# One of v's last two projection products moved by half a key block at the end of each image's fourth head

## The chip, the cores and the metric

The kernel runs on 1 core of one Trainium2 chip. The metric is device time in microseconds (us): the median over runs of the whole program on that core. Before the change it is 3168.52 us (3 runs, 3167.76 to 3169.66).

## The reference, cut to what matters

The input x has 16 images of 512 channels and 32x32 positions (n = 1024), all in float32. Each image goes through group normalisation, a 1x1 convolution to q, k and v, attention with 4 heads of 128 channels over the 1024 positions, a 1x1 convolution of the result, and the residual sum.

```python
xn = ((xg - mu) * rsqrt(var + EPS)).reshape(b, c, h, w) * gamma + beta
q, k, v = split(einsum('oc,bchw->bohw', qkv_w, xn) + qkv_b, 3, axis=1)
q, k, v = to_heads(q), to_heads(k), to_heads(v)        # b, 4 heads, 1024, 128
attn = softmax(einsum('bhnd,bhmd->bhnm', q, k) * dh ** -0.5, axis=-1)
out = einsum('bhnm,bhmd->bhnd', attn, v).transpose(0, 1, 3, 2).reshape(b, c, h, w)
return x + einsum('oc,bchw->bohw', proj_w, out) + proj_b
```

## The kernel before, in words

**The main loop.** `fast_path` (L187) walks over 16 images x 4 heads x 8 key blocks of 128 keys, 512 steps in all (L1245). A step has two halves of 512 queries. In each half TensorE gets the scores of this step (`scores`, L862, written `s<-qk,qk` in the profile), then the weighted sum of the step before (`weighted_sum`, L935, `po<-p,v`), then some projection products taken from a list. ScalarE turns the scores into exponentials (L868, tile `p`), and VectorE adds those up over the key blocks (L881, tile `tot`). The denominators of a head come from `tot` (L890 to L904) in the second step of the next head (the call is at L1257).

**The projections in between.** The projections that feed other heads and the next image are spread over the halves. A projection (q and k for a pair of heads, v, or the output) is a two-level Strassen product (`two_levels`, L539). The outer level gives four groups, `OUTER = ((1, 5), (2, 6), (7, 4), (3,))` (L183), so that groups 0 to 2 do two outer products side by side and group 3 does one. Inside each group stand the seven inner products of `strassen` (L488), in the order 1, 2, 6, 5, 7, 4, 3 (L184). In group 3 an inner product is one 128x256 product, which the trace shows as two matmuls of 256 columns; a score or a weighted sum of a half shows as two matmuls of 512.

**The PSUM tiles of a group.** `x` takes products 1, 6, 7 and 4 one on top of the other, and ScalarE copies it out after each (tiles `p1`, `u2`, `u3`, and the result c21 itself, L644). One `y` bank takes product 2. Another `y` bank takes product 5 and, on top of it, product 3. Between these two VectorE has to read that bank:

```python
def p7():
    mm(t["x"], 7, False)
    kept_copy("u3")
    out_("c22", t["y"], t["u3"])
def p3():
    mm(t["y"], 3, False)
    out_("c12", t["y"], t["u2"])
```

So the eviction c22 (L646, `v_r<-v_y,v_u` for v) waits for the copy u3, and product 3 waits for that eviction. The eviction c12 reads the same bank after product 3.

**Who does which product when.** During the fourth head (`h` = 3) of images 0 to 14, the 28 inner products of v for the next image run. `products` (L971) cuts the list into pieces by the table `SIZES` (L967), one piece for each half from the head's first one on, and the loop takes one piece per half behind the weighted sum (L1271). The table for this head, `SIZES[NB - 1]`, has 15 pieces; a head has 16 halves. The list is in the staggered order of `staggered` (L983), whose last seven entries are group 3 alone. The next head, the first of the next image, has the products of q and k of the second pair (`qk_groups(b + 1, 1)`), with the table `SIZES[NB]`.

**What follows v's products on VectorE and POOL.** After c12 the last pieces of v are formed: a sum (L784, `vt`), a transpose (L787, `vu`), a write to memory (L795, `vd<-vu`, on POOL's queue) and, when both halves of 128 rows are there, four reads back (L800, `v<-vd`, POOL too). The piece that hangs on the last product is v's second half of the first pair of heads: key blocks 4 to 7 of the next image's first two heads.

**Order.** The program order is a scheduler's, with urgency marks: the evictions, exponentials and copies are marked urgent. Each engine works its own instructions off in the order of the build, and waits on semaphores.

Of the kernel before, what the change touches and what calls it, by code (L numbers as in the profile page):

```python
# [115 lines left out]
def attention_block(  # L116
# [35 lines left out]
    with ExitStack() as fast:  # L152
        fast_path(fast, tc, x, sources, out, consts, flag, dims)
# [33 lines left out]
def fast_path(ctx, tc, x, sources, out, consts, flag, dims):  # L187
# [7 lines left out]
    B, C, N, NCC, NH2, NB, GC, SCALE = dims  # L195
# [757 lines left out]
    def bias_of_v(o):  # L953
# [3 lines left out]
        for c in range(NCC):  # L957
# [7 lines left out]
        )  # L965

    SIZES = {NB: (2, 2, 2, 1, 2, 2, 2, 1, 2, 2, 1, 2, 2, 2, 1, 2),  # L967
             NB - 1: (2, 2, 2, 2, 2, 2, 2, 2, 2, 1, 2, 2, 2, 1, 2)}
    halfway = []

    def products(plan, units, last):  # L971
# [444 lines left out]
```

## Time and profile before

| what | value |
| --- | --- |
| median of 3 runs | 3168.52 us (3167.76 to 3169.66) |
| the profiled execution's own time | 3169.05 us |
| its span in the trace | 3167.1 us |
| share of the span: TensorE, VectorE, ScalarE, POOL | 99%, 84%, 46%, 16% |
| mean granted TensorE clock | 0.999 |
| scores (L862): busy | 1047.0 us, 2048 matmuls |
| weighted sums (L935): busy | 1046.4 us, 2048 matmuls |

The span is the time from the first to the last instruction in the trace; the profiled execution's own time is 1.95 us longer. A matmul's end in the trace is modelled, and matmuls overlap, so that the distance between two starts says more of their cost than the duration in a row. In rows of the timeline the columns are the start, the time to the end of the last of the merged instructions, the engine, the line, the operation with its output and inputs, the count, and in brackets the idle time before it and what ended it. Engines are PE (TensorE), PEld (its weight loads), DVE (VectorE), ACT (ScalarE) and POOL.

### The profile page before, as it was taken

How to read it: one execution, taken by the hardware profiler on the slowest of the kernel's cores; microseconds unless marked ns; L12 is line 12 of the kernel's file. 1: busy time of each engine (PE TensorE's matmuls, PEld its weight loads, DVE VectorE, ACT ScalarE, POOL GpSimd, SP SyncE). 2: the span in 40 equal slices, each digit the busy share in tenths (PEclk: the TensorE clock that was granted, in tenths of full speed). 3: DMA queues.
4: the chain of work that ended last, by engine and by line, in shares of the span. 5: the costliest groups of instructions: out<-in, count | busy, mean ns of one | idle time of the engine just before them, and what ended most of it. 6: DMA issues, size and time to landing. Idle time of an engine off the chain costs nothing.

```text
span 3167.1 us, 34165 instructions
## 1 busy us (share of the span) xinstructions
PE 3142.6 (99%) x10442; PEld 2199.9 (69%) x10442; DVE 2659.1 (84%) x4687; ACT 1446.1 (46%) x2651; POOL 497.8 (16%) x897
## 2 busy tenths in 40 slices
PE   9999999999999999999999999999999999999999
PEld 7566767677776776767767677676776767767764
DVE  9878979788897888978889787997879978789785
ACT  3535435354353543535435454353534535345333
POOL 0011121111211112111121111211112120121200
PEclk9999999999999999999999999999999999999999
DMA  5554554546545455554555545555455554555631
GB/s 177 187 185 157 184 177 149 172 150 199 167 158 174 143 194 173 167 161 147 196 166 169 167 147 192 168 171 161 148 187 170 174 175 139 180 164 177 192 117 48
DMA packets 210668, 524.83 MB, mean 166 GB/s; under 512 B 32176, under 2 KB 65456, under 8 KB 210480
## 3 DMA queue, kind: packets, MB, share of 16 engines
q1 hardware_dynamic: 133088, 282.39, 29.0%
q0 software_dynamic: 64000, 204.54, 18.8%
q10 hardware_dynamic: 13392, 35.66, 3.3%
q8 instruction: 86, 1.41, 0.2%
q14 instruction: 102, 0.84, 0.1%
HBM read 389.30 MB, written 133.17 MB: 165 GB/s over the span
## 4 chain that ended last, share of the span: by engine, by line
PE 90%; DVE 8%; DMA 1%; issue 1%; ACT 0%; SPq 0%; POOL 0%; ACTq 0%; DVEq 0%; POOLq 0%
PE s L862 26%; PE po L935 25%; PE qk_x L622 12%; PE qk_y L622 9%; PE pp_x L622 6%; PE v_x L622 4%; PE pp_y L622 4%; PE v_y L622 4%; DVE tot L881 1%; DVE vu L787 1%; DVE v_r L646 1%; DVE qk_t L590 1%; DVE vt L784 1%; DVE v_r L695 1%; DVE o L946 1%
## 5 line engine op out<-in xcount | busy, mean ns | idle before, releaser
L862 PE MATMUL s<-qk,qk 128*128 128x512 f32 x2048 | 1047.0, 593 | 0.3 <-DVE qk L730 0.3
L935 PE MATMUL po<-p,v 128*128 128x512 f32 x2048 | 1046.4, 593 | 0.7 <-ACT p L868 0.7
L868 ACT ACTIVATE p<-s 128x512 f32<-128x512 f32 x1024 | 611.1, 597 | 868.8 <-PE s L862 832.4
L935 PEld LDWEIGHTS po<-p,v 128*128 128x128 f32 x2048 | 616.4, 301 | 376.8 <-issue 256.0
L881 DVE TENSOR_TENSOR tot<-tot,p 128x1024 f32<-128x1024 f32 x385 | 469.9, 1220 | 152.7 <-ACT p L868 152.6
L862 PEld LDWEIGHTS s<-qk,qk 128*128 128x128 f32 x2048 | 389.1, 190 | 76.7 <-issue 19.9
L622 PEld LDWEIGHTS qk_x<-qk_t,w 128*128 128x128 f32 x1344 | 254.4, 190 | 152.7 <-issue 91.1
L622 PE MATMUL qk_x<-qk_t,w 128*128 128x256 f32 x1344 | 353.9, 380 | 0.1
L502 ACT COPY qk_u<-qk_x 128x512 f32<-128x512 f32 (+1 forms) x256 | 136.6, 533 | 240.2 <-PE qk_x L622 227.9
L795 POOL DMA_DIRECT2D vd<-vu x120 | 66.4, 555 | 969.8 <-DVE vu L787 885.7
L646 DVE TENSOR_TENSOR qk_r<-qk_y,qk_u 128x512 f32<-128x512 f32 (+1 forms) x256 | 158.6, 620 | 35.6 <-ACT qk_u L502 21.3
L596 POOL DMA_DIRECT2D kept_t<-qk_t x240 | 129.9, 542 | 273.7 <-DVE qk_t L590 203.6
L622 PEld LDWEIGHTS pp_x<-pp_t,w_proj 128*128 128x128 f32 x630 | 119.7, 190 | 71.8 <-issue 43.0
L646 DVE TENSOR_TENSOR v_r<-v_y,v_u 128x512 f32<-128x512 f32 (+1 forms) x120 | 76.1, 634 | 110.3 <-ACT v_u L502 80.1
L622 PE MATMUL pp_x<-pp_t,w_proj 128*128 128x256 f32 x630 | 165.4, 379 | 0.0
L622 PE MATMUL v_x<-v_t,w_v 128*128 128x256 f32 x630 | 165.3, 379 | 0.0
L846 POOL DMA_DIRECT2D out_y<-y x120 | 65.4, 545 | 606.8 <-DVE groups L293 399.3
L622 PEld LDWEIGHTS v_x<-v_t,w_v 128*128 128x128 f32 x630 | 119.7, 190 | 59.0 <-issue 34.4
L800 POOL DMA_DIRECT2D v<-vd x240 | 140.4, 592 | 96.0 <-issue 44.5
L622 PE MATMUL qk_y<-x,w 128*128 128x256 f32 x512 | 142.0, 379 | 0.0
L730 DVE SCALAR_TENSOR_TENSOR qk<-qk_r,qkb_sb,qk_r 128x512 f32<-128x512 f32 x192 | 137.9, 746 | 1.6
L644 ACT COPY qk_r<-qk_x 128x512 f32<-128x512 f32 (+1 forms) x128 | 68.3, 533 | 147.7 <-PE qk_x L622 112.5
(214 smaller groups left out, 4458.2 us busy)
## 6 DMA issues: line engine op xcount, KB each, us to landing
w<-kept SPq DMA_DIRECT2D x90, 512.0 KB, 3.9
kept_t<-qk_t POOLq DMA_DIRECT2D x180, 256.0 KB, 3.2
v_t<-kept_t SPq DMA_DIRECT2D x180, 256.0 KB, 2.8
w<-kept SPq DMA_DIRECT2D x90, 384.0 KB, 3.7
rinv<-row ACTq DMA_DIRECT2D x63, 512.0 KB, 4.8
x<-in_x POOLq DMA_DIRECT2D x60, 512.0 KB, 4.4
vd<-vu POOLq DMA_DIRECT2D x120, 256.0 KB, 2.9
v<-vd POOLq DMA_DIRECT2D x240, 128.0 KB, 3.7
```

The source lines that it names most:

```text
L502: nc.scalar.copy(t[n][:, :width], t["x"][:, :width])
L596: nc.gpsimd.dma_start(t, to)
L622: nc.tensor.matmul(acc[:, ts(i, Q)], have["w"][t][:, i, slot, :], inner(i, bn), start=(first and i == 0), stop=True, skip_group_check=True,)
L644: nc.scalar.copy(dst, view(a))
L646: nc.vector.tensor_add(dst, view(a), view(c))
L730: nc.vector.scalar_tensor_tensor(st[b, h][:, ts(half, HALF)], a, qkb_sb[:, i : i + 1], c, ALU.add, ALU.add)
L795: nc.gpsimd.dma_start(rows[which][ts(h, P), :], u)
L800: nc.gpsimd.dma_start(vs[b, pair][ts(q, BLK), half].rearrange("m h (k i) j -> m (h k) (i j)", k=n), rows[which].rearrange("(k m) (q e) -> ...
L862: nc.tensor.matmul(sc, ks[b, h][:, ts(j, P)], qs[b, h][:, ts(half, HALF)], start=True, stop=True)
L868: exps[s] = nc.scalar.activation(ps[s][:, ts(half, HALF)], sc, AF.Exp, scale=SCALE)
L881: added[b, h, j] = nc.vector.tensor_add(tot[b, h][:, i], tot[b, h][:, i], ps[s][:, i])
L935: summed = nc.tensor.matmul(po[half], v_block(b, h, j), ps[s][:, i], start=(j == 0), stop=(j == NB - 1),)
```

## The change

One entry of the table is split in two: the last piece of two products becomes two pieces of one.

```diff
     SIZES = {NB: (2, 2, 2, 1, 2, 2, 2, 1, 2, 2, 1, 2, 2, 2, 1, 2),
-             NB - 1: (2, 2, 2, 2, 2, 2, 2, 2, 2, 1, 2, 2, 2, 1, 2)}
+             NB - 1: (2, 2, 2, 2, 2, 2, 2, 2, 2, 1, 2, 2, 2, 1, 1, 1)}
```

Before, products 4 and 3 of v's group 3 stand together in the first half of the eighth key block (half 15 of 16). After, product 4 stands there, and product 3 in the second half (half 16), behind the scores and the weighted sum of that half. This is so in 15 of the 16 images. On TensorE nothing else moves. On VectorE the eviction of product 3 and the two `vt`, `vu` pairs behind it come later in the order, and a few instructions of other tiles come before them. On POOL the four instructions of v's last piece keep their places, with other tile numbers. SyncE's order is the same, and so is ScalarE's.

## The prediction

> **What bounds the kernel now.** I read the page's first part, then the waits of TensorE, then its timeline around the one wait that repeats, and last VectorE's timeline there. The page:
>
> ```profile
> PE 3142.6 (99%) x10442; PEld 2199.9 (69%) x10442; DVE 2659.1 (84%) x4687; ACT 1446.1 (46%) x2651; POOL 497.8 (16%) x897
> ```
>
> TensorE has work nearly all the time, so the end is set by the sum of its matmuls and the gaps between them. The gaps are few. The table of TensorE's waits (total us, times, longest us), its first three lines:
>
> ```profile
> PE v_y L622 <- DVE v_r L646: 13.3, 15, 1.1
> PE warm L1157 <- DVE avg L248: 1.5, 1, 1.5
> PE qk_x L622 <- DMA w<-kept: 1.4, 1, 1.4
> ```
>
> One wait occurs 15 times: a v product that writes `v_y` waits for VectorE's eviction `v_r`. All other waits listed occur once. The timeline of TensorE at the fourth of the 15 places shows which product it is:
>
> ```profile
> 823.57 0.59 PE L622 MATMUL v_x<-v_t,w_v 128*128 128x256 f32 x2
> 824.00 1.02 PE L862 MATMUL s<-qk,qk 128*128 128x512 f32 x2
> 824.86 1.02 PE L935 MATMUL po<-p,v 128*128 128x512 f32 x2
> 825.72 0.59 PE L622 MATMUL v_x<-v_t,w_v 128*128 128x256 f32 x2
> 827.17 0.70 PE L622 MATMUL v_y<-x,w_v 128*128 128x256 f32 x2 [0.86 <-DVE v_r L646]
> 827.71 1.02 PE L862 MATMUL s<-qk,qk 128*128 128x512 f32 x2
> 828.57 1.02 PE L935 MATMUL po<-p,v 128*128 128x512 f32 x2
> ```
>
> These are product 7 alone (823.57), a half's score and weighted sum, product 4 (825.72) and product 3 (827.17). Product 3 stands in the queue ahead of the next score, so the score waits with it. VectorE in the same stretch:
>
> ```profile
> 825.56 1.23 DVE L881 TENSOR_TENSOR tot<-tot,p 128x1024 f32<-128x1024 f32 x1
> 826.68 0.44 DVE L646 TENSOR_TENSOR v_r<-v_y,v_u 128x256 f32<-128x256 f32 x1
> 827.02 1.11 DVE L787 STREAM_TRANSPOSE vu<-vt 128x512 f32<-128x512 f32 x1
> 827.95 0.70 DVE L784 TENSOR_TENSOR vt<-v_r 128x512 f32<-128x512 f32 x1
> 828.54 0.43 DVE L590 TENSOR_TENSOR qk_t<-x,qk_t 128x256 f32<-128x256 f32 x1
> 828.87 0.43 DVE L646 TENSOR_TENSOR v_r<-v_y,v_u 128x256 f32<-128x256 f32 x1
> 829.20 1.11 DVE L787 STREAM_TRANSPOSE vu<-vt 128x512 f32<-128x512 f32 x1
> ```
>
> The eviction that releases product 3 is the one at 826.68 (c22). It sits behind a running sum and ends at 827.12; product 3 starts at 827.17. No row has idle time: VectorE is full here.
>
> **The change, part by part.**
>
> *The stall that goes.* From product 4's start to the next score's start is 827.71 - 825.72 = 1.99 us. Without a wait, two 256-column matmuls take 0.43 (823.57 to 824.00), four take 0.86. So the stall is 1.13, of which the row shows 0.86 as idle; the other 0.27 is the overlap lost before the gap and the slower first matmul behind it. Over the 15 places the distance is 1.99 six times, between 2.00 and 2.03 eight times, and 2.22 once; the sum is 30.22. Less 15 x 0.86 = 12.90, it is 17.3 us.
>
> Summed by the idle column it would be 13.3 us only. [...]
>
> *Whether product 3 still waits.* Its new start is 825.72 + 0.43 (product 4) + 0.86 + 0.86 (score and weighted sum) = 827.87, which is 0.70 behind the 827.17 at which it was let go. At the place with the longest stall the new start is 2195.83 + 2.15 = 2197.98, against 2197.51: 0.47 to spare. The instructions in between wait for nothing new: the score takes the bank of the score two halves back, whose exponential is over, and that weighted sum reads a `p` that is a step old. So no rest of the stall stays.
>
> *The split itself.* Product 3 now runs alone between a weighted sum and a score. Product 7 at 823.57 stands exactly so and costs 0.43, the same as in a pair; I take 0. Bounds: below, nothing can be gained, for the number of matmuls stays the same; above, a restart as behind the stall, 0.27 x 15 = 4.0 us.
>
> *VectorE's order.* The same instructions run, in another order. Behind the `qk_t` at 828.54 stand now: `vu` (0.94 from start to start), one `qk_t` (0.34), the running sum (1.12), and only then c12's eviction. So c12 starts at 828.87 + 2.40 = 831.27 and ends by 831.7, 2.4 later than before. It then waits for no one: product 3 ends at about 828.5. The running sum comes a little earlier, at 830.15; its exponential ended 1.66 after its score started (827.71, 829.37), so now at 826.15 + 1.66 = 827.81. VectorE, having had no idle time, works the same list off in the same time.
>
> *What is late next.* TensorE runs 1.13 earlier against an unmoved VectorE. The next products that wait for VectorE, all in the first q/k group of the next head: product 5 needs the bank that c12 frees. It ran at 835.45, now 834.32: 2.6 to spare. Product 3 of that group needs its own c22:
>
> ```profile
> 842.30 0.68 DVE L646 TENSOR_TENSOR qk_r<-qk_y,qk_u 128x512 f32<-128x512 f32 x1
> 842.90 0.68 DVE L335 TENSOR_TENSOR ot<-o,ot 128x512 f32<-128x512 f32 x1
> 843.50 1.22 DVE L879 TENSOR_TENSOR tot<-p,p 128x1024 f32<-128x1024 f32 x1
> 845.12 0.69 DVE L646 TENSOR_TENSOR qk_r<-qk_y,qk_p 128x512 f32<-128x512 f32 x1 [0.40 <-PE qk_y L622]
> ```
>
> c22 ends at 842.98; the product ran at 844.92, now 843.79: **0.81 to spare**, the thinnest cover. In the last of the 15 places it is 2997.09 against 2996.79, 0.30. From 845.12 on VectorE waits for TensorE (0.40, and 0.17 and 0.80 in the next rows), so it catches up there and the gain is safe.
>
> ScalarE and POOL: ScalarE's transfer of the reciprocals is held behind an exponential that moves from 840.82 to 839.69, and the reciprocal ends at 839.26. POOL's first `vd` write of v's last piece moves from 833.34 to about 835.5, behind the later `vu`; the second stays at about 839.4, and the reads of v follow that one (839.97 to 844.62), as before. They land within 5.1 us, by 849.7; the weighted sum that needs them is at 862.99 - 1.13. SyncE's weight loads follow TensorE's releases.
>
> *Sum.* -17.3 + 0 = -17.3 us. The profiled execution took 3169.05 us (span 3167.1), which gives 3151.7; it lies 0.53 above the median of the runs, which gives 3151.2. I predict **3151.5**.
>
> **The rivals.**
>
> *Only the idle time comes back.* The 0.27 per place stays, because a product of its own breaks the flow as the stall did: 3169.05 - 13.3 = 3155.8. Against it: product 7 alone costs 0.43.
>
> *The wait moves to the next group's product 3.* VectorE is full from 824 to 843, and its evictions stand behind one another. If the new order costs it X in this stretch, TensorE loses X - 0.81 per image: at X = 1.4, 15 x 0.59 = 8.9 us, 3160 us. For it: the cover is 0.30 to 0.81. Against it: the list is the same, and nothing in it gets a later input. [...]
>
> *Slower: VectorE is held by a `vd` write.* A `vu` transpose takes a buffer whose write must have landed. In the last of the 15 places this row of VectorE shows a wait of 0.44 for it. If the later `vu` ran into that in every image, TensorE would stand at the next product 3, at X - 1.94 more than before per image (0.81 plus the 1.13 won). It is slower by over 0.2% (0.42 per image) from X = 2.36; at X = 3 it is 15 x 1.06 = 16 us, 3184 us. For it: these writes take 2.9 us to land in the median and 6.0 at most. Against it: the waiting `vu` stands where it stood, and the write before it is issued 0.3 earlier.
>
> *The change doesn't do what it says.* If product 3 were still let go late, or the sixteenth piece were not taken, nothing changes: 3168.5. Against it: the order of the build shows product 3 behind the score and weighted sum of the last half in all 15 images, and its release 0.70 ahead.
>
> **How the numbers follow.** Forecast 0.74, by itself 3149 to 3154: spread of the runs and a few tenths per place. Only the idle time 0.08; the wait moves on 0.07; no effect 0.05; slower 0.06. The range reaches from 3148.5 over the split's upper bound (3155.8) into the third case, to 3159 (half a microsecond lost per image, 7.5 us); beyond lie some 0.15. Measurement can tell about 0.2% (6.3 us) from no change: faster by more is the forecast, the second case and most of the third, 0.88; within it 0.06; slower 0.06.
>
> **What would show it.** TensorE's waits lose the line `v_y <- v_r`; from product 4's start to the next score is 0.43; product 3 alone takes 0.43 between weighted sum and score; c12 starts 2.4 behind its old place while the reciprocal keeps its distance from the first eviction; VectorE's idle 0.40 ahead of `qk_r` is gone and TensorE has no wait for VectorE at `qk_y`. A new line `qk_y <- DVE qk_r` with 15 entries, or a `vu <- DMA vd` wait, would prove me wrong, and so would a product 3 that takes 0.7.

## The result and the profile after

| | before | after |
| --- | --- | --- |
| median of 6 runs | 3169.59 us (3167.76 to 3171.86) | 3150.84 us (3150.11 to 3154.2) |
| the profiled execution's own time | 3169.05 us | 3151.40 us |
| its span | 3167.1 us | 3149.4 us |
| chain that ended last: TensorE, VectorE | 90%, 8% | 97%, 2% |

The ratio is 0.9942, with a 95% interval of 0.9929 to 0.9955. The kernel became 0.6% faster, 18.8 us by the medians and 17.65 us by the two profiled executions.

The page's line of engines, after:

```profile
PE 3137.7 (100%) x10442; PEld 2200.8 (70%) x10442; DVE 2658.2 (84%) x4687; ACT 1444.6 (46%) x2651; POOL 497.8 (16%) x897
```

TensorE's waits, after (total us, times, longest us), the first three lines:

```profile
PE qk_x L622 <- DMA w<-kept: 1.7, 1, 1.7
PE warm L1157 <- DVE avg L248: 1.5, 1, 1.5
PE qk_x L622 <- DVE qk_t L590: 0.8, 1, 0.8
```

The instruction counts are the same and VectorE works as long as before; TensorE's longest list entry, the 15 waits of `v_y` for `v_r`, is gone. What is left occurs once each. The third line is new; it lies between 100 and 200 us, in the first image, ahead of the first moved product.

TensorE at the fourth place, after (start, time to the end of the merged instructions, engine, line, operation, count):

```profile
820.09 0.59 PE L622 MATMUL v_x<-v_t,w_v 128*128 128x256 f32 x2
820.52 1.02 PE L862 MATMUL s<-qk,qk 128*128 128x512 f32 x2
821.38 1.02 PE L935 MATMUL po<-p,v 128*128 128x512 f32 x2
822.24 0.59 PE L622 MATMUL v_x<-v_t,w_v 128*128 128x256 f32 x2
822.67 1.02 PE L862 MATMUL s<-qk,qk 128*128 128x512 f32 x2
823.53 1.02 PE L935 MATMUL po<-p,v 128*128 128x512 f32 x2
824.39 0.59 PE L622 MATMUL v_y<-x,w_v 128*128 128x256 f32 x2
824.82 1.02 PE L862 MATMUL s<-qk,qk 128*128 128x512 f32 x2
```

Product 4 (822.24) is followed by the score after 0.43. Product 3 (824.39) stands alone behind the weighted sum and takes 0.43 too, with no idle time in brackets. VectorE there:

```profile
823.22 0.42 DVE L646 TENSOR_TENSOR v_r<-v_y,v_u 128x256 f32<-128x256 f32 x1
823.56 1.07 DVE L787 STREAM_TRANSPOSE vu<-vt 128x512 f32<-128x512 f32 x1
824.49 0.67 DVE L784 TENSOR_TENSOR vt<-v_r 128x512 f32<-128x512 f32 x1
825.08 0.40 DVE L590 TENSOR_TENSOR qk_t<-x,qk_t 128x256 f32<-128x256 f32 x1
825.41 1.10 DVE L787 STREAM_TRANSPOSE vu<-vt 128x512 f32<-128x512 f32 x1
826.35 0.41 DVE L590 TENSOR_TENSOR qk_t<-x 128x256 f32<-128x256 f32 x1
826.68 1.21 DVE L881 TENSOR_TENSOR tot<-tot,p 128x1024 f32<-128x1024 f32 x1
827.81 0.41 DVE L646 TENSOR_TENSOR v_r<-v_y,v_u 128x256 f32<-128x256 f32 x1
```

c22 (823.22) now ends at 823.64, 0.75 ahead of product 3. c12 has slid behind the running sum: it starts 4.59 behind c22, before it was 2.19. No engine stands idle for it.

### The profile page after: what moved, and what is told of

Its sections match the earlier page's. It is cut to its first block, busy times and chain, and to the rows that moved or that the text cites. A ratio compares the mean times of both kernels' runs of the same rounds, so it can differ in the third digit from the quotient of the medians.

```text
span 3149.4 us, 34165 instructions
## 1 busy us (share of the span) xinstructions
PE 3137.7 (100%) x10442; PEld 2200.8 (70%) x10442; DVE 2658.2 (84%) x4687; ACT 1444.6 (46%) x2651; POOL 497.8 (16%) x897
## 4 chain that ended last, share of the span: by engine, by line
PE 97%; DVE 2%; DMA 0%; issue 0%; POOL 0%; ACT 0%; SPq 0%; DVEq 0%; POOLq 0%
PE s L862 27%; PE po L935 27%; PE qk_x L622 12%; PE qk_y L622 9%; PE pp_x L622 6%; PE v_x L622 6%; PE pp_y L622 4%; PE v_y L622 4%; PE lx L1034 0%; DVE qk_t L590 0%; PE ly L1034 0%; PE warm L1157 0%; DVE qk L730 0%; DVE qk_r L646 0%; DMA st_a<-in_proj_wT 0%
```

## The experiments

The theory: the whole gain is product 3's wait for the eviction c22, and it lasts as long as the next eviction that TensorE needs (the c22 of the next head's first q/k group) has cover. The rival that had to be told apart from it: what helps is the even filling of the last halves, one product in each.

**1. The wait taken away, no product moved.** The kernel before, with c22 of v's group 3 put in front on VectorE. The `vt` sum of v's c21 and the running sum that the order had ahead of it, and sums for a q/k group of the next head, are held behind it (the main lines of the edit):

```diff
-                        nc.vector.tensor_add(dst, view(a), view(c))
+                        ins = nc.vector.tensor_add(dst, view(a), view(c))
+                        if site == "v" and g == len(OUTER) - 1 and which == "c22":
+                            early[b] = ins
...
-        if not (h == 1 and j == 6 and 0 < b < B - 1):
+        if not (j == 6 and (h == 1 and 0 < b or h == 3) and b < B - 1):
             running_sum(s, half)
...
+        if s < steps and h == 3 and j == 6 and b < B - 1:
+            with tc.issue_after(early[b + 1].ins):
+                running_sum(s, 1)
...
+                if site == 1 and g == 1 and b in early:
+                    order.enter_context(tc.issue_after(early[b].ins))
...
+            late_ = tc.issue_after(early[b].ins) if b in early else nullcontext()
```

The last line stands in v's `finish` around `vt` and `vu`, and in v's group 3 the two pieces of c21 are taken up behind products 7 and 4, one each, not both behind product 2.

> Kernel before, products 4 and 3 still together in half 15, but VectorE's eviction c22 of v's group 3 is put ahead of the running sum and of the pieces of v that stood in front of it. Theory (the gain is the wait of product 3 for c22): c22 can start at about 825.3 instead of 826.7 on the scale of the fourth place, ends 0.4 to 0.5 ahead of product 3's own start at 826.15, TensorE's line v_y waits for v_r is gone, and the time is 3151 to 3154, 15 to 18 us below the kernel before, with no product moved. Rival (what helps is one product in each of the last two halves): nothing, 3167 to 3171.

Measured: 3152.88 us, ratio 0.995 (0.9936 to 0.9963). TensorE at the fourth place of this kernel:

```profile
820.65 0.59 PE L624 MATMUL v_x<-v_t,w_v 128*128 128x256 f32 x2
821.08 1.02 PE L875 MATMUL s<-qk,qk 128*128 128x512 f32 x2
821.94 1.02 PE L948 MATMUL po<-p,v 128*128 128x512 f32 x2
822.79 0.59 PE L624 MATMUL v_x<-v_t,w_v 128*128 128x256 f32 x2
823.23 0.59 PE L624 MATMUL v_y<-x,w_v 128*128 128x256 f32 x2
823.66 1.02 PE L875 MATMUL s<-qk,qk 128*128 128x512 f32 x2
```

and VectorE's eviction with what now follows it:

```profile
822.35 0.46 DVE L648 TENSOR_TENSOR v_r<-v_y,v_u 128x256 f32<-128x256 f32 x1
822.68 0.72 DVE L797 TENSOR_TENSOR vt<-v_r 128x512 f32<-128x512 f32 x1
823.27 1.26 DVE L894 TENSOR_TENSOR tot<-tot,p 128x1024 f32<-128x1024 f32 x1
```

Products 4 and 3 still stand together in half 15, and run back to back (822.79, 823.23), because c22 ended at 822.81, 0.42 ahead (0.41 to 0.43 at the 15 places). The line `v_y <- v_r` is gone from TensorE's waits here too. The same gain without the move: the wait is the cause, and the even filling is not needed.

**2. Both remedies.** The changed table on top of experiment 1:

```diff
-             NB - 1: (2, 2, 2, 2, 2, 2, 2, 2, 2, 1, 2, 2, 2, 1, 2)}
+             NB - 1: (2, 2, 2, 2, 2, 2, 2, 2, 2, 1, 2, 2, 2, 1, 1, 1)}
```

> The changed kernel with the same earlier eviction on top. Theory: the two remedies cure one wait, so they do not add: 3149 to 3153, as the changed kernel within 2 us. Rival (VectorE's order and the split are worth something each on their own): about 3134, 17 us below the changed kernel.

Measured: 3152.98 us, ratio 0.9947 (0.9934 to 0.9961). The remedies do not add: one wait, cured once. The 2.1 us above the changed kernel lie inside the interval, about 4 us to each side, and experiment 1 alone has 3152.88.

**3. Both products late.** Half 15 empty, the pair in half 16:

```diff
-             NB - 1: (2, 2, 2, 2, 2, 2, 2, 2, 2, 1, 2, 2, 2, 1, 1, 1)}
+             NB - 1: (2, 2, 2, 2, 2, 2, 2, 2, 2, 1, 2, 2, 2, 1, 0, 2)}
```

> The two products stay a pair, but both in half 16, none in half 15 (the last entries of the table are 1, 0, 2). Theory: product 3 starts where the changed kernel has it, 0.7 behind its release, so 3149 to 3153 although the halves are filled unevenly. Rival (even filling): 3158 or more, since half 15 is empty and half 16 has two. A second rival, that product 4's later copy holds something: a new line of waits on TensorE, some tenths for each of 15 places.

Measured: 3150.96 us, ratio 0.9943 (0.9929 to 0.9956), and no new line among the waits. TensorE at the fourth place:

```profile
825.12 1.02 PE L862 MATMUL s<-qk,qk 128*128 128x512 f32 x2
825.97 1.02 PE L935 MATMUL po<-p,v 128*128 128x512 f32 x2
826.83 0.59 PE L622 MATMUL v_x<-v_t,w_v 128*128 128x256 f32 x2
827.26 0.59 PE L622 MATMUL v_y<-x,w_v 128*128 128x256 f32 x2
827.70 1.02 PE L862 MATMUL s<-qk,qk 128*128 128x512 f32 x2
```

The pair takes 0.87, one product alone 0.43: how the two halves are filled costs nothing here. What counts is that product 3 comes a score and a weighted sum later.

**4 to 7. How far the cover reaches.** c22 of the next head's first q/k group is done several times over (the same sum into the same place), once on the changed kernel and once on the kernel before:

```diff
-                        nc.vector.tensor_add(dst, view(a), view(c))
+                        for _ in range(2 if (site, g, which) == (1, 0, "c22") and b > 0 else 1):
+                            nc.vector.tensor_add(dst, view(a), view(c))
```

The 2 is a 3 in the third and fourth kernel.

> The changed kernel, where VectorE does the eviction c22 of the first q/k group of the next head (the one that the next product 3 waits for, covered by 0.76 us) twice in a row, in images 1 to 15. With what the order puts between them the last one ends 1.2 us later. Theory (that eviction is the next wait): TensorE stands 0.45 to 0.75 us at each of 15 places (the excess over the cover, and up to 0.27 for the restart), 7 to 12 us, 3157 to 3163, with a new line qk_y waits for qk_r of 15 entries. Rival (VectorE has room there, 84% busy): 3151.

> The kernel before with the same doubled eviction. Theory: its cover there is 1.94 us, 1.2 is inside, so nothing: 3167 to 3171. Together with the split kernel's run the gain of the change shrinks from 18 to 6 to 12 us.

> The changed kernel with that eviction three times; the running sum falls between the second and the third, so the last ends 2.95 us later. Theory: 2.2 us beyond the cover and up to 0.27 for the restart at each of 15 places, 33 to 37 us, 3184 to 3189. Rival (room on VectorE): 3151 to 3155.

> The kernel before with that eviction three times. Theory: 2.95 less the cover of 1.94 is 1.0, with the restart 1.0 to 1.3 at each of 15 places, 15 to 20 us, 3184 to 3189: the same as the changed kernel with the same load, within 3 us, so that nothing of the change's gain is left, because TensorE's time at this place is then set by VectorE alone.

| that eviction | changed kernel | kernel before |
| --- | --- | --- |
| once | 3150.84 | 3169.59 |
| twice | 3162.75, ratio 0.9982 (0.9973 to 0.9992) | 3169.25, ratio 1.0003 (0.9994 to 1.0013) |
| three times | 3201.78, ratio 1.0107 (1.009 to 1.0124) | 3187.03, ratio 1.0059 (1.0042 to 1.0075) |

The first row is that of the first table. Ratios are against the kernel before, run on the same chip as the loaded kernels (3168.61 us). Twice: the changed kernel loses 11.9 us and the kernel before nothing that can be told. The longest entry among TensorE's waits in the changed kernel with the doubled eviction, and the product that has it:

```profile
PE qk_y L622 <- DVE qk_r L647: 6.0, 15, 0.4
```

```profile
842.64 0.59 PE L622 MATMUL qk_y<-xt,w 128*128 128x256 f32 x2
843.66 1.13 PE L622 MATMUL qk_y<-x,w 128*128 128x256 f32 x4 [0.42 <-DVE qk_r L647]
844.63 1.02 PE L863 MATMUL s<-qk,qk 128*128 128x512 f32 x2
```

By starts the place costs 844.63 - 842.64 - 0.43 - 0.86 = 0.70, while its idle column says 0.42: 15 x 0.70 = 10.5 of the 11.9 us. So the next wait is where the prediction put it, and the cover has the size it had.

Three times: the kernel before came out as expected (18.4 us above itself). The changed kernel did not: 3201.8 instead of 3184 to 3189. Its longest entry among the waits is the expected one:

```profile
PE qk_y L622 <- DVE qk_r L647: 32.0, 15, 2.2
```

The granted TensorE clock is what differs: its mean over the execution is 0.995, and 0.999 in the loaded kernel before. Stretches of 4 us behind the wait, at the second, third and fifth place (busy us of TensorE, its weight loads, VectorE, ScalarE and POOL, with the instructions in brackets; then PEclk, the granted clock, the DMA share and GB/s):

```profile
456.22:460.22 4.00, 4.00 (x8) 2.21 (x9) 1.32 (x3) 0.60 (x1) 1.88 (x4) 0.57 0.92 241
654.88:658.88 4.00, 4.00 (x15) 3.02 (x16) 2.46 (x3) 0.85 (x2) 2.38 (x6) 1.00 0.86 238
1050.53:1054.53 4.00, 4.00 (x8) 2.43 (x9) 1.24 (x2) 0.32 (x1) 1.48 (x3) 0.57 0.79 206
```

At 8 of the 15 places the mean clock fell (0.57 to 0.61 over these 4 us), and the stretch holds 8 matmuls instead of 15. TensorE at the second place shows the price:

```profile
456.22 1.54 PE L622 MATMUL qk_y<-x,w 128*128 128x256 f32 x4 [2.07 <-DVE qk_r L647]
457.56 1.91 PE L863 MATMUL s<-qk,qk 128*128 128x512 f32 x2
459.26 1.50 PE L936 MATMUL po<-p,v 128*128 128x512 f32 x2
460.60 1.03 PE L622 MATMUL qk_x<-qk_t,w 128*128 128x256 f32 x4
```

The score takes 1.70 from start to start, 0.86 elsewhere, so it ran at half the rate. The matmuls of these four rows take 5.24 (the next one starts at 461.46); at the last of the 15 places, where the clock stayed at 1.00, the same ones take 3.55 (3030.85 to 3034.40). The drop of the clock cost 1.69 us there. At five more of the 8 places the four rows take 5.23 or 5.24, and at three more of the 7 others 3.54 or 3.55. Eight drops then cost 13.5, an estimate from these rows; 3201.8 - 13.5 = 3188.3, inside the expected range and 1.3 us from the loaded kernel before. So the expectation's other half holds, that with so late an eviction nothing of the gain is left; what it lacked is a cost that comes behind the stall.

## Why the prediction was right

*The stall and its sum.* 17.3 us were forecast, 17.65 were measured between the profiled executions. From the first place to the last, product 4's start moved from 238.48 and 2979.01 to 238.44 and 2962.85: the 14 images between took 16.12 us less, 1.15 each. The starts of before gave 16.2 for the same 14. The idle column would have given 13.3 in all, which lies outside the measured interval of the ratio (14.3 to 22.5 us): it leaves out a quarter of the stall. At the fourth place of before, product 4's row ends 0.16 behind the 826.15 at which product 3 would have followed it, and product 3 then took 0.54 instead of 0.43; the two make up the 0.27 that the column lacks. Experiment 4 shows the same, 0.70 by starts against 0.42 idle. To go by the starts was the author's choice before the run; the 17.65 and the 0.70 bear it out.

The forecast time, 3151.5, lies 0.7 us above the measured median. It rested on a median of 3 runs before; with 6 runs that median is 1.1 us higher, so the gain by the medians is 18.8 us and not 17.3. The sum is rather to be held against the 17.65 of the two executions.

*No rest of the stall.* Right: c22 ends 0.75 ahead of product 3 at the fourth place (0.70 forecast), and the wait is absent at all 15; where the stall had been longest, 0.52 is left (0.47 forecast).

*The split at no cost.* Right: 0.43 alone, and experiment 3's pair is no better.

*VectorE's order.* Right in every step that was priced: c12 comes 2.40 later (2.4), and the reciprocal starts 12.33 behind c22, before 12.30. POOL's first `vd` write of v's last piece is issued at 832.39 + 3.46 = 835.85 on the old scale, by c22's start (about 835.5 forecast). The eviction c12, now queued behind the running sum, held up no one. One more eviction slid that the prediction had not named, the first of the next q/k group (`qk_r<-qk_y,qk_p`): it starts 10.36 behind c22, before 8.95, and TensorE shows no wait for it.

*What is late next.* Right, and tested. At the changed kernel's fourth place that c22 ends at 839.55, and product 3 of the q/k group starts at 840.31: 0.76 to spare (0.81 forecast). Over the 15 places it is 0.42 to 0.76; the forecast had 0.30 as the least, at the last place, which now has 0.72. VectorE's idle 0.40 behind it is gone, as forecast:

```profile
838.87 0.68 DVE L646 TENSOR_TENSOR qk_r<-qk_y,qk_u 128x512 f32<-128x512 f32 x1
839.47 0.68 DVE L335 TENSOR_TENSOR ot<-o,ot 128x512 f32<-128x512 f32 x1
840.07 1.22 DVE L879 TENSOR_TENSOR tot<-p,p 128x1024 f32<-128x1024 f32 x1
841.21 0.68 DVE L646 TENSOR_TENSOR qk_r<-qk_y,qk_p 128x512 f32<-128x512 f32 x1
```

*The rivals.* Only the idle time: refuted by the starts. The wait moves on: not here, but experiment 4 shows its place, and that 1.2 us more on VectorE bring it. The `vd` write: no such wait among TensorE's, and VectorE's one wait of 0.44 for it is gone after; it was not made to occur more often, so its price stays an argument. No effect: refuted.

## What to carry to other kernels

Where one engine is full, look for the wait that repeats, and price it by the distance between starts, not by the idle column: here the starts gave 17.3 us and the column 13.3, and 17.65 were measured. A product that waits for an eviction in its own bank was cured here from either end, by moving the product back (3150.84 us) or the eviction forward (3152.88); both gave the same gain, and the two together no more (3152.98). Then measure the cover of the next wait on the same engine: here 0.42 to 0.76 us stood between a gain of 18 us and losing it. An eviction that ended 1.2 us later took back 11.9 us, and one that ended 2.9 us later took back more than all.

## What had not been expected of the hardware

In the changed kernel with the tripled eviction (experiment 6), TensorE stalled about 2.1 us at each of the 15 places (32.0 us in all by the idle column, 2.25 at most). At 8 of them the granted clock fell behind the stall, to a mean of 0.57 to 0.61 over 4 us, and at the six of them that were read the score took 1.66 to 1.71 us from start to start, not 0.86; at the other 7 the clock stayed at 1.00. At the same place of the loaded kernel before (experiment 7) the stalls were 0.82 to 1.73 us: the clock was 1.00 at the five places where it was read, and the score took 0.85 or 0.86 at the other ten.

The length of the stall alone does not say where the clock fell: behind 2.07 us at 456.22 it did, behind 2.25 us at 2635.13 it did not. What decided it no run here shows. With the clock, the waits cost more than they show: 51 us for 15 waits that show 32.0 as idle.
